# Gates on GpSimd's weight work and slot copies in a fused attention and feed-forward kernel

## The chip, the cores and the metric

The kernel runs on one core of a Trainium2 chip. A core has a matrix engine (TensorE, PE in the profile), a vector engine (VectorE, DVE), a scalar engine (ScalarE, ACT), GpSimd (POOL), and SyncE (SP), which here only issues transfers. Each engine works through its own list of instructions in the order in which the program wrote them, and waits at an instruction until the semaphores it names have come. The metric is the device time of one execution in microseconds; lower is better.

## The reference

The input is 4 sequences of 1024 tokens with 256 features. A block of attention with 16 heads of 16 features and a feed-forward block of three ternary layers follow each other, each between two layer norms and with a residual:

```python
x = L0_attn_x
x = x + _layernorm(_L0_attn_ref(_layernorm(x, axis=-1), L0_attn_Wqkv, L0_attn_Wout), axis=-1)
x = x + _layernorm(_L0_ffn_ref(_layernorm(x, axis=-1), ...), axis=-1)
# attention
scores = jnp.einsum('bhqd,bhkd->bhqk', q, k) * scale
attn = _stable_softmax(scores)          # exp(clip(x - max, -50, 50)) / (sum + 1e-6)
out = jnp.einsum('bhqk,bhkd->bhqd', attn, v)
# feed-forward
h = jax.nn.silu(_tlin(x, w1_w, w1_s)) * _tlin(x, w2_w, w2_s)
h = jax.nn.gelu(_tlin(h, h1_w, h1_s), approximate=False)
h = jax.nn.gelu(_tlin(h, h2_w, h2_s), approximate=False)
return _tlin(h, w3_w, w3_s)
```

## The kernel before

**Two stages.** Attention runs from the start to about 573 us, the feed-forward block from there to the end. The changed lines all act in attention.

**Units and tiles.** Attention is cut into 32 units (b, g, h): sequence b of 4, group g of 4 heads, half h of the queries. In this text unit n is counted from 0, so that n = 8 b + 2 g + h. A unit has 16 score tiles (c, u): 8 key tiles c of 128 tokens, and two pairs of heads u. A score tile is two matmuls (`exponentials`, L554) and one exponential of 128x1024 on ScalarE (L555). The exponentials of a key tile are then weighed with the values in a matmul that accumulates over the 8 key tiles (`weigh`, L562, tile `acc`, one PSUM buffer). At the end of a unit VectorE transposes `acc` to `o` (L824), and the next unit's first `acc` matmul has to wait for that. The exponentials stand in a ring of 8 tiles, and VectorE takes a running maximum over a part of them (`rise`, L574, tile `top`), so that a place in the ring comes free when both have read it.

**Rounds.** The loop at L1464 writes the program round by round: 3 score tiles are made, then the key tiles that are ready are weighed (three halves of a tile, or four where the weighing has fallen behind, and never past a unit's end), then `side.take` at L1501 writes other work. There are 16 rounds in three units. The variable `weighed` tells which score tile is weighed next, and `tiles[weighed][3]` is its c.

**Other work.** `Side` holds chains of `Step`s. A step comes out at the first `take` that is at least `gap` takes after the step before it in its chain, if its `ready()` says yes. Steps that use TensorE come out one at a time, the others freely; within a `take` the chains go in the order in which they were added. So `Side` decides only where in each engine's list an instruction stands. The engine then runs it as soon as its semaphores allow, which can be long before TensorE is at that round.

**What GpSimd does in attention.**

- `round_weights` (6 blocks of w1, w2, w3) and then `round_corners` (16 corners of h1 and h2) form one chain. A corner has three steps: `load` (two transfers into the tile `w`, L309), `plain` (two copies L319 and L320 and a store, L312) and `sums` (four additions or subtractions L327 to L330 and a store). The gaps are 2, 3 and 1. The tile `w` has one buffer, and so has `wr`, which both `plain` and `sums` write: the first addition has to wait until the store of `plain` has landed.
- `slots` copies the values of four heads into `vaug` (L532), two units ahead of their use. `unit_end` writes it, before it adds the chain of `stack`.
- `stack` copies the queries and keys of a group into the tiles `sq` and `sk` that the score matmuls read. These are 32 transfers of 64 KB (L500) in six steps of 6, 6, 6, 6, 6 and 2, one step to a take; every third transfer is issued by GpSimd and the others by SyncE. Of the GpSimd share, the steps have 2, 2, 2, 2, 2 and 1. The last eight transfers, in the last two steps, fill the query stack of u = 1. The first step waits until the queries and keys have been made (`later["qk"]`, `later["qk1"]`), which is late for groups 2.
- The inverse roots of the layer norms (`rstd`, L107) and small squares (`sum`, L432), both behind a VectorE instruction.

The chain of the weights is added before all chains of `stack` but the first, so within one take the weights come first.

Of the kernel before, what the change touches and what calls it, by code (L numbers as in the profile page):

```python
# [73 lines left out]
class Step:  # L74


    def __init__(self, run, gap=0, tensor=True, heavy=False, work=0, split=False):
        self.run, self.gap, self.tensor, self.heavy, self.work, self.split = run, gap, tensor, heavy, work, split
        self.ready = lambda: True


class Norms:
# [61 lines left out]
def tile_fast(ctx: ExitStack, tc: tile.TileContext, x, wqk, wv, wo, w1, w1s, w2, w2s, h1, h1s, h2, h2s, w3, w3s, out, bad):  # L144
# [5 lines left out]
    NT = S // P  # L150
# [62 lines left out]
    with ExitStack() as actx, ExitStack() as rctx:  # L213
# [60 lines left out]
        work = actx.enter_context(tc.tile_pool(name="work", bufs=2, side="right"))  # L274

        def misc(name):
            return ps_misc.tile([P, NQ], F32, tag="misc", name=name)

        def round_weights(n, c):

            st = {}

            def rows(w):
                return w[c * P : (c + rows_at_once[n]) * P, :].rearrange("(i p) d -> p i d", p=P)

            def load():
                st["w"] = work.tile([P, WIDE], F32, tag="w", name="w", bufs=1)
                nc.gpsimd.dma_start(out=st["w"].rearrange("p (i d) -> p i d", i=rows_at_once[n]), in_=rows(weights[n]))

            def cast():  # L290
                st["r"] = work.tile([P, WIDE], F32R, tag="wr", name="wr", bufs=1)
                nc.gpsimd.tensor_copy(st["r"], st["w"])
                nc.gpsimd.dma_start(out=rows(rounded[n]).bitcast(F32), in_=st["r"].bitcast(F32).rearrange("p (i d) -> p i d", i=rows_at_once[n]))

            return [Step(load, 2, False), Step(cast, 4, False)]

        made_factors = [0]

        def round_corners(n, c, x):


            st = {}
            half = NQ // 2

            def load():
                st["w"] = work.tile([P, WIDE], F32, tag="w", name="w", bufs=1)
                rows = weights[n].rearrange("(j c p) (i x n) -> c x p j i n", j=2, p=P, i=2, x=2)[c, x]
                for j in range(2):
                    nc.gpsimd.dma_start(out=st["w"].rearrange("p (j i n) -> p j i n", j=2, i=2)[:, j], in_=rows[:, j])  # L309

            def store(r, k0, k1):
                nc.gpsimd.dma_start(  # L312
                    out=factors[n][k0:k1, :, c, x * half : (x + 1) * half].rearrange("k p n -> p k n").bitcast(F32),
                    in_=r.bitcast(F32).rearrange("p (k n) -> p k n", n=half)[:, : k1 - k0],
                )

            def plain():
                r = work.tile([P, WIDE], F32R, tag="wr", name="wr", bufs=1)
                nc.gpsimd.tensor_copy(r[:, 0:half], st["w"][:, 0:half])  # L319
                nc.gpsimd.tensor_copy(r[:, half : 3 * half], st["w"][:, 2 * half : 4 * half])  # L320
                store(r, 0, 3)

            def sums():
                r = work.tile([P, WIDE], F32R, tag="wr", name="wr", bufs=1)
                s1, s2, s3, s4 = (r[:, k * half : (k + 1) * half] for k in range(4))
                a11, a21, a12, a22 = (st["w"][:, k * half : (k + 1) * half] for k in range(4))
                nc.gpsimd.tensor_tensor(s1, a21, a22, ALU.add)  # L327
                nc.gpsimd.tensor_tensor(s2, s1.bitcast(F32), a11, ALU.subtract)
                nc.gpsimd.tensor_tensor(s3, a11, a21, ALU.subtract)
                nc.gpsimd.tensor_tensor(s4, a12, s2.bitcast(F32), ALU.subtract)  # L330
                store(r, 3, 7)
                made_factors[0] += 1

            return [Step(load, 2, False), Step(plain, 3, False), Step(sums, 1, False)]

        def by_slots(o, w, i, **flags):

# [176 lines left out]
        def stack(b, g):  # L514

            outstanding.append((b, g))

            def done():
                stacked[g % 2] = b, g
                outstanding.remove((b, g))  # L520

            turns = (nc.sync, nc.gpsimd, nc.sync)
            runs = [copy for w in (1, 0) for copy in copies(g, w)]
            steps = few([lambda copy=copy, queue=turns[i % len(turns)]: copy(queue) for i, copy in enumerate(runs)], 2 * len(turns))
            steps[0].ready = lambda: later["qk" if g < GPT else "qk1"] == b
            return steps + [Step(done, 0, False)]

        def slots(b, g, t0=0, t1=NT, engine=nc.gpsimd):


            def run():
                engine.tensor_copy(  # L532
                    vaug[g % 2][:, t0:t1, :, 0:DH], cv[:, t0:t1, HPG * DH * g : HPG * DH * (g + 1)].rearrange("p t (h e) -> p t h e", e=DH)
                )
                slotted[g % 2] = b, g, t1

            return run
# [3 lines left out]
        tiles = [(b, g, h, c, u) for b in range(B) for g in range(NG) for h in range(NH) for c in range(NT) for u in range(2)]  # L541
# [173 lines left out]
        class Side:  # L715


            def __init__(self):
                self.first, self.rest, self.slot = [], [], 0
                self.room, self.open, self.tired = 0.0, None, False  # L720
# [58 lines left out]
        side = Side()  # L779
# [41 lines left out]
        def unit_end(b, g, h):  # L821

            o = both.tile([P, NQ], F32, tag="o", name="o", bufs=2)
            nc.vector.transpose(o, accs[b, g, h])  # L824
            unit = side.add((divide_last if (b, g) == (B - 1, NG - 1) else divide)(g, h, o, tops[b, g, h]), True)
            if b and not g:

                unit[0][-1].ready = lambda: not any(step.tensor for step in ends[b - 1, h][0])
            if g == NG - 1:
                last = ending(b, h, to_scalar if (b, h) == (B - 1, NH - 1) else to_vector)  # L830
                unit[0].extend(last)
                ends[b, h] = unit
            if h < NH - 1:
                return

            n, at = g + 2, b
            if n >= NG:
                n, at = n - NG, b + 1
            if b == B - 1 and g == NG - 2:
                side.add([Step(lambda q=q: load_factor(q), 2 if q else 0, False) for q in range(SLOTS // 2)])  # L840
            if at < B:
                put = Step(slots(at, n), 0, False)
                if at > b:
                    later["chain"][0].append(put)
                else:
                    put.run()
                side.add(stack(at, n))
            if g == NG - 3 and b + 1 < B:
                later["chain"][0].extend(later["rest"])
            elif g == NG - 3:  # L850
                chunks = [(n, [c]) for n in ("w1", "w2") for c in range(DC)]
                loads = [Step(lambda n=n, c=c: load_weights(n, c), 2 if n == "w1" else 1, False) for n, c in chunks]

                loads[0].ready = lambda: not later["flags"][0]
                loads[DC].ready = lambda: not outstanding
                side.add(loads)
                second = prepare(1, to_vector)
                second[-DC].ready = lambda: not outstanding
                side.add([Step(lambda: None, 3, False)] + prepare(0, to_vector) + second)
            if g == NG - 1:  # L860
                begin(b + 1)
# [11 lines left out]
        def load_weights(n, chunks=None):  # L873
            for c in range(len(homes[n])) if chunks is None else chunks:
                nc.sync.dma_start(out=homes[n][c].bitcast(F32), in_=rounded[n][c * P : (c + 1) * P, :].bitcast(F32))

        def load_factor(q):


            if q >= B * 2 * len(order):  # L880
                return
            n, k = square[q // len(order) % 2], order[q % len(order)]
            for i, t in enumerate(ring_of[q % SLOTS]):
                nc.sync.dma_start(out=t.bitcast(F32), in_=factors[n][k, :, 2 * i : 2 * i + 2, :].bitcast(F32))
# [567 lines left out]
        begin(0)  # L1452
        side.add(stack(0, 1) + few(load_rest(), 1))
        side.add([s for k in blocks for s in round_weights(*k)] + [s for k in corners for s in round_corners(*k)])
        made = seen = weighed = half = 0

# [7 lines left out]
        while weighed < len(tiles):  # L1464
            n = end = made
# [3 lines left out]
            if made == len(tiles):  # L1469
                n = made  # L1470
# [274 lines left out]
```

## Time and profile before

| | us |
|---|---|
| median of 3 runs | 1183.34 (1180.86 to 1184.16) |
| profiled execution, device time | 1187.39 |
| profiled execution, span from first to last instruction | 1185.6 |
| attention, first unit's end to last unit's end | 49.7 to 573.5 |
| busy in 45 to 573: PE, ACT, DVE, POOL | 509.1, 485.6, 396.3, 255.1 |
| last store of a corner of the weights begins | 455.67 |

The profiled execution took 1187.39 us, 4.05 us above the median of the runs. "Busy" is the time in which an engine had an instruction under way; for POOL it includes the issuing of its transfers. A wait line reads "engine, tile, line <- what was waited for: us in total, times, longest". A timeline row reads "start in us from the first instruction, us, engine, line, operation, tiles written <- read, shape, count", with the idle time before it in brackets, and what ended it.

### The profile page before, as it was taken

Reading aid. Unit: us, or ns where it says so; the run is one execution under the profiler, and the core shown is the slowest. Engines: PE = TensorE matmul, PEld = TensorE weight load, DVE = VectorE, ACT = ScalarE, POOL = GpSimd, SP = SyncE. Lnnn points to the kernel's source line nnn. Section 1 sums busy time; section 2 is a strip of 40 time slices with the busy share of each in tenths; the row PEclk is TensorE's granted clock in tenths of the full one; section 3 lists DMA queues with packets and bytes.
Section 4 is the critical chain, followed back from the end, with each engine's and each line's share of the span. In section 5 each row is a group of like instructions: output and inputs, shape, how many; then the busy total and the mean of one; then the engine's idle time right before and its main releaser. Section 6 shows DMA issues by size and latency. Waiting matters only on the chain.

```text
span 1185.6 us, 21591 instructions
## 1 busy us (share of the span) xinstructions
PE 1150.1 (97%) x8122; PEld 715.4 (60%) x8122; DVE 847.0 (71%) x1503; ACT 892.9 (75%) x1061; POOL 301.0 (25%) x458
## 2 busy tenths in 40 slices
PE   8999999999999999999999999999999999999996
PEld 3333333334333343333578889888898888988886
DVE  3576578986877876787785756868668686685856
ACT  3899899988998889999467565676756767566664
POOL 6364265674765563220000000000000000000000
PEclk9999999999999999999999999999999999999999
DMA  5865565666646565463304342254622545225421
GB/s 144 221 176 156 142 187 138 185 182 168 164 140 174 153 171 145 100 158 117 108 26 141 119 161 70 91 183 134 196 71 92 176 141 194 73 91 180 138 72 39
DMA packets 78737, 163.68 MB, mean 138 GB/s; under 512 B 14752, under 2 KB 40992, under 8 KB 78624
## 3 DMA queue, kind: packets, MB, share of 16 engines
q1 hardware_dynamic: 62752, 120.05, 34.6%
q0 software_dynamic: 15200, 41.50, 11.8%
q8 instruction: 66, 1.08, 0.4%
q10 hardware_dynamic: 672, 0.66, 0.2%
q14 instruction: 47, 0.39, 0.1%
HBM read 98.71 MB, written 29.88 MB: 108 GB/s over the span
## 4 chain that ended last, share of the span: by engine, by line
PE 77%; ACT 8%; DVE 7%; issue 3%; DMA 2%; SPq 1%; POOL 1%; ACTq 0%; POOLq 0%; DVEq 0%
PE ph L1072 34%; PE acc L562 13%; PE pg L993 9%; PE s L554 8%; ACT e L555 7%; PE pz L1172 5%; PE p L339 3%; PE py L339 2%; PE pv L339 2%; DVE top L574 1%; DVE st L97 1%; SPq L500 1%; PE fpt L936 1%; DMA w<-in_w_dram 1%; DVE xn L140 0%
## 5 line engine op out<-in xcount | busy, mean ns | idle before, releaser
L555 ACT ACTIVATE e<-s 128x1024 f32<-128x1024 f32 x512 | 484.3, 1041 | 44.0 <-PE s L554 36.8
L562 PE MATMUL acc<-e,vaug 128*32 128x512 f32 (+1 forms) x2552 | 255.6, 515 | 1.9 <-DVE o L824 1.8
L107 POOL TENSOR_TENSOR rstd<-ve,minus_half 128x4 f32<-128x4 f32 (+1 forms) x33 | 38.4, 1163 | 679.6 <-DVE ve L105 679.6
L554 PE MATMUL s<-sq,sk 64*128 64x512 f32 x1024 | 187.1, 443 | 18.2 <-ACT e L555 14.6
L554 PEld LDWEIGHTS s<-sq,sk 64*128 64x128 f32 x1024 | 88.1, 185 | 152.6 <-ACT e L555 112.6
L1072 PE MATMUL ph<-hi,sq 128*128 128x512 f32 x448 | 175.7, 392 | 0.0
L1072 PE MATMUL ph<-lo,sq 128*128 128x512 f32 x448 | 174.7, 390 | 0.0
L1072 PE MATMUL ph<-lo,sk 128*128 128x512 f32 x448 | 174.5, 390 | 0.0
L1072 PE MATMUL ph<-hi,sk 128*128 128x512 f32 x448 | 174.4, 389 | 0.0
L574 DVE TENSOR_TENSOR top<-top,e 128x512 f32<-128x512 f32 x192 | 138.8, 723 | 14.2 <-ACT e L555 8.1
L562 PEld LDWEIGHTS acc<-e,vaug 128*32 128x32 f32 x2552 | 66.0, 109 | 122.0 <-issue 107.2
L967 DVE TENSOR_TENSOR lo<-g,hi 128x1024 fp32r<-128x1024 f32 x48 | 58.8, 1224 | 52.4 <-ACT hi L963 52.4
L1072 PEld LDWEIGHTS ph<-lo,sk 128*128 128x128 f32 x448 | 84.2, 188 | 17.5
L1072 PEld LDWEIGHTS ph<-hi,sk 128*128 128x128 f32 x448 | 84.1, 188 | 17.5
L1072 PEld LDWEIGHTS ph<-lo,sq 128*128 128x128 f32 x448 | 84.2, 188 | 17.1
L1072 PEld LDWEIGHTS ph<-hi,sq 128*128 128x128 f32 x448 | 84.1, 188 | 17.1
L1060 ACT ACTIVATE c<-ph,h_scale 128x512 f32<-128x512 f32 x64 | 40.5, 685 | 52.0 <-PE ph L1072 52.0
L995 ACT ACTIVATE sg<-pg,w_scale 128x512 f32<-128x512 f32 x64 | 44.0, 688 | 44.4 <-PE pg L993 38.0
L967 DVE TENSOR_TENSOR lo<-c,hi 128x1024 fp32r<-128x1024 f32 x48 | 58.2, 1220 | 24.2 <-ACT hi L963 24.2
L339 PE MATMUL p<-xT,wqk_sb 128*32 128x512 f32 x512 | 65.7, 593 | 0.5 <-ACT xT L342 0.5
L996 DVE SCALAR_TENSOR_TENSOR g<-pg,w_scale,sg 128x512 f32<-128x512 f32 x64 | 47.8, 748 | 19.9 <-ACT sg L995 19.9
L1172 PE MATMUL pz<-w_sb,lo 128*128 128x256 f32 x256 | 61.6, 283 | 0.0
(199 smaller groups left out, 1848.2 us busy)
## 6 DMA issues: line engine op xcount, KB each, us to landing
sq<-h_f SPq DMA_DIRECT2D x56, 512.0 KB, 4.0
sk<-h_f SPq DMA_DIRECT2D x56, 512.0 KB, 4.7
w<-in_h_dram POOLq DMA_DIRECT2D x32, 256.0 KB, 5.2
h_f<-wr POOLq DMA_DIRECT2D x16, 512.0 KB, 4.0
x<-in_h_dram SPq DMA_DIRECT2D x16, 512.0 KB, 3.5
top_d<-top SPq DMA_DIRECT2D x30, 256.0 KB, 2.6
folded<-top_d SPq DMA_DIRECT2D x30, 256.0 KB, 3.2
h_f<-wr POOLq DMA_DIRECT2D x16, 384.0 KB, 3.6
```

The source lines that it names most:

```text
L339: nc.tensor.matmul(o[j : j + SLOT, :], w[:, j : j + SLOT], i, **flags)
L554: nc.tensor.matmul(s[:, a, :], stacks[1, g % 2, u][r, c * P : (c + 1) * P], stacks[0, g % 2, u][r, h * NQ : (h + 1) * NQ], start=True, sto ...
L555: nc.scalar.activation(pair(k)[:, u], s, AF.Exp)
L562: nc.tensor.matmul(acc[SLOT * i : SLOT * (i + 1), q0:q1], vaug[g % 2][:, c, i, :], pair(k)[:, i // 2, i % 2, q0:q1], start=c == 0 and q0 = ...
L574: nc.vector.tensor_max(top, top if c > 1 else pair(k - 2)[:, :, :, 0:P], pair(k)[:, :, :, 0:P])
L967: nc.vector.tensor_sub(self.lo[i].t, self.raw[i].t, self.hi[i].t.bitcast(F32))
L993: nc.tensor.matmul(p[:, k, :], homes[n][d][:, m * P : (m + 1) * P], half[:, d, :], start=d == j == 0, stop=d == DC - 1 and j == 1)
L995: nc.scalar.activation(sg, p[:, 0, :], AF.Silu, scale=scales["w1"][:, m : m + 1])
L996: nc.vector.scalar_tensor_tensor(x[i, h][c // 2].t[:, c % 2, :], p[:, 1, :], scales["w2"][:, m : m + 1], sg, ALU.mult, ALU.mult)
L1060: nc.scalar.activation(o.t[:, j, :], (o.t if src is None else src)[:, j, :], AF.Gelu, scale=scale[:, m : m + 1])
L1072: nc.tensor.matmul(p[:, j, :], w, half, start=start and c == n == 0, stop=c == HC // 2 - 1 and n == 1, skip_group_check=True,)
L1172: yield c, lambda half=half, c=c, n=n: nc.tensor.matmul(p[:, j, :D], half[:, t * P : (t + 1) * P], homes["w3"][c], start=c == order[0] and ...
```

## The change

A step can be given a `ready` when it is made. The new helper `inside(lead, rest)` says yes while the tile weighed next has a c from `lead` to 8 - `rest`, and always once all tiles are weighed. The casts of blocks, `plain` and the slot copies may come out at c from 0 to 5, `sums` at c from 1 to 4. The slot copy that `unit_end` used to write at once becomes a chain of its own ahead of the chain of `stack`; its gap is now 1 in place of 0, also where it stands at the end of the prologue's chain.

```diff
-    def __init__(self, run, gap=0, tensor=True, heavy=False, work=0, split=False):
+    def __init__(self, run, gap=0, tensor=True, heavy=False, work=0, split=False, ready=lambda: True):
         self.run, self.gap, self.tensor, self.heavy, self.work, self.split = run, gap, tensor, heavy, work, split
-        self.ready = lambda: True
+        self.ready = ready
...
+        def inside(lead, rest):
+            return lambda: weighed == len(tiles) or lead <= tiles[weighed][3] <= NT - rest
+
         def round_weights(n, c):
...
-            return [Step(load, 2, False), Step(cast, 4, False)]
+            return [Step(load, 2, False), Step(cast, 4, False, ready=inside(0, 3))]
...
-            return [Step(load, 2, False), Step(plain, 3, False), Step(sums, 1, False)]
+            return [Step(load, 2, False), Step(plain, 3, False, ready=inside(0, 3)), Step(sums, 1, False, ready=inside(1, 4))]
...
             if at < B:
-                put = Step(slots(at, n), 0, False)
+                put = Step(slots(at, n), 1, False, ready=inside(0, 3))
                 if at > b:
                     later["chain"][0].append(put)
                 else:
-                    put.run()
+                    side.add([put])
                 side.add(stack(at, n))
```

## The prediction

> **What bounds the kernel now.** I read the page first, then the busy time by stage, the waits between 45 and 573 us, and the timelines of the places that these name.
>
> ```profile
> PE 1150.1 (97%) x8122; PEld 715.4 (60%) x8122; DVE 847.0 (71%) x1503; ACT 892.9 (75%) x1061; POOL 301.0 (25%) x458
> ...
> POOL 6364265674765563220000000000000000000000
> ...
> PE 77%; ACT 8%; DVE 7%; issue 3%; DMA 2%; SPq 1%; POOL 1%; ACTq 0%; POOLq 0%; DVEq 0%
> ```
>
> TensorE is busy for 97% and carries 77% of the chain that ended last; GpSimd carries 1%. Its row is filled up to slice 19 only, so the change can act in attention alone. There (45 to 573 us, 528 us) PE is busy for 102.53 + 146.39 + 144.51 + 115.71 = 509.1 us, and ACT for 485.6: PE has about 19 us of idle time, and that is the most that any reordering could win. The waits say who owns it (engine, what for, total us, times, longest):
>
> ```profile
> PE s L554 <- ACT e L555: 13.2, 37, 1.2
> PE s L554 <- DMA sq<-cq1lo: 2.3, 2, 1.8
> PE acc L562 <- DVE o L824: 1.8, 4, 1.0
> ...
> ACT e L555 <- DVE top L574: 5.2, 4, 1.9
> ```
>
> No line has POOL as the one waited for. GpSimd reaches PE in two ways only. First through VectorE, when both want the same operands' port: VectorE is late, then ScalarE, then PE. Second through the transfers that GpSimd issues: the wait for `sq` is one for a stack copy. Both have an instance in the timelines. The first, at the start of units 12 and 21 (ACT):
>
> ```profile
> 240.81 3.77 ACT L555 ACTIVATE e<-s 128x1024 f32<-128x1024 f32 x4 [1.69 <-DVE top L574]
> ...
> 397.93 3.77 ACT L555 ACTIVATE e<-s 128x1024 f32<-128x1024 f32 x4 [1.87 <-DVE top L574]
> ```
>
> At both, GpSimd was at the four operations of `sums` (236.67 to 240.1, 395.01 to 398.4). PE's own idle rows there, found in its list of gaps, are 1.00 us at 241.89 and 1.21 at 399.00, its two longest behind ACT. The second, at the end of unit 19 (PE), and the same place one sequence later, near the end of unit 27 (POOL, SP, PE):
>
> ```profile
> 372.29 1.24 PE L554 MATMUL s<-sq,sk 64*128 64x512 f32 x6 [1.83 <-DMA sq<-cq1lo]
> ```
>
> ```profile
> 495.05 0.57 POOL L432 TENSOR_TENSOR sum<-sum 128x1 bf16<-128x1 f32 x1 [8.70 <-DVE sum L431]
> 495.56 0.53 POOL L500 DMA_DIRECT2D sk<-ck1hi  x1
> 496.08 0.96 POOL L500 DMA_DIRECT2D sq<-cq1hi  x2
> 497.04 0.48 POOL L500 DMA_DIRECT2D sq<-cq1lo  x1
> 497.51 0.48 POOL L500 DMA_DIRECT2D sq<-cq1hi  x1
> 497.99 0.96 POOL L500 DMA_DIRECT2D sq<-cq1lo  x2
> ```
>
> ```profile
> 503.39 2.42 SPq L500 DMA_DIRECT2D sq<-cq1lo  x2
> ```
>
> ```profile
> 507.24 1.81 PE L554 MATMUL s<-sq,sk 64*128 64x512 f32 x6
> ```
>
> Here the stack of (b 3, g 2) is copied. SyncE issues the last two transfers at 503.4 and 504.0, they land in 3.5 us, and the matmuls of the first u = 1 tile start at 508.4. GpSimd's share was issued by 499. So the deadline is met by SyncE with nothing to spare, and GpSimd has some 9 us left.
>
> **What the Trainium skill says.** "SBUF — State Buffer", Who interferes with whom: a VectorE instruction with two SBUF inputs contends with a GpSimd instruction that reads SBUF, and the second to start is held until the first ends. The trace agrees: a `top` takes 649 ns at least and up to 1229, and the operations of L328 to L330 take 730 ns undisturbed and 1180 beside a `top`. "Trainium Kernel Development and Optimization", Key Constraints: transfers of all issuing engines run on the same 16 DMA engines, and issuing from several only saves issue time. In the trace a stack copy costs GpSimd 0.49 us to issue.
>
> **The change part by part.** No instruction is added or removed, and weights and slots have `work` 0 and no TensorE, so the lists of PE, ACT, DVE and SP stay as they are. Only POOL's list is reordered.
>
> *Where the steps go.* By the loop's rule of three or four halves, takes come at c = 0, 2, 4, 5, 7 in units with n divisible by 3, at 0, 2, 3, 5, 6 in the next and at 0, 1, 3, 4, 6, 7 in the one after. The chain of weights starts at the first take. Counting gaps gives for the kernel before one corner in 6 takes, the first `sums` at unit 7, c 5 and the last at unit 24, c 4; the trace has the first at 160.65 (unit 7 runs from 150.7 to 166.4) and the last at 452.44 (unit 24 from 445.5 to 462.2), so the count holds. With the gates I get the `sums` at (unit, c) = (8,1) (9,2) (10,3) (11,4) (13,2) (14,3) (15,4) (17,1) (18,2) (19,3) (20,4) (22,2) (23,3) (24,4) (26,1) (27,2). Five corners are held by 3 takes: the last store moves by 15 takes, 15 x 3.1 us (528 us over 171 takes) = 46 us, from 455.7 to about 502 to 506. The first h factor is asked for at unit 29's end, 545 us, so the weights themselves are not late.
>
> *Slot copies.* In the middle of a sequence they go from the unit's end to the take just behind it (c 0 is allowed): some 0.6 us of work moved by nothing that counts, as `vaug` is used 16 us later. Those for the next sequence move by one take (3.1 us); the tightest was done at 297.85 and needed at 306. Cost 0.
>
> *Gain at the two VectorE stalls.* `sums` at (12,0) and (21,0) go. Worth the PE gaps, 1.00 + 1.21 = 2.2 us (up to ACT's 3.6). But `sums` at (18,2) and (8,1) now stand behind a slot copy that waits for the unit's end, so they run in its first 4 us. At unit 18 the first two `top`s and the product `on` have two SBUF inputs; two collisions at 0.4 to 0.5 us (1.18 - 0.69) make 0.8 us, at unit 8 half as much: +1.3. `sums` at (26,1) delays a `rstd` by some 1.7 us; behind it VectorE has idle gaps of 0.93 and 2.96 us that take it up. Together -0.9 (bounds -4 and +1).
>
> *Stack of (3,2), end of unit 27.* `plain` now comes out at (27,0) and `sums` at (27,2), in front of stack steps 4 and 5 (counted from 0; SyncE's order around the write and read of `top_d` puts these at (27,2) and (27,4)). POOL's list: the `sum` waits for VectorE until 495.05, as before, and stack step 2 is issued by 496.6. `plain`: 1.5 us to its store at 498.1 (1.2 to 2.3 in most corners). Store 0.8 and stack step 3 1.0: to 499.9. `sums` must wait for that store to land: from a store's issue to the first addition, the corners that wait show 2.93 to 4.74, mean 3.6: 501.7. Four operations, with the wait before the store, 4.0 (3.5 to 4.6): 505.7. Store 0.8: 506.5. Step 4 is issued from 506.5 to 507.5, step 5 until 508.0. A stack copy issued right behind such a store landed in 3.0 to 6.3, mostly 4.2: 507.5 + 4.2 = 511.7, where 508.4 was the start: PE is held for 3.3 to 3.5 us (0.6 with every short end, 7.9 with every long one). PE is in order, ACT has no scores left, so the time is lost whole. What is late next: all of unit 28 on, equally.
>
> *Stack of (2,2), end of unit 19.* The same with `plain` (19,2) and `sums` (19,3) in front of steps 4 and 5. The stack step before is issued by 357.8, `plain`'s store at 359.5, `sums` from 363.2 to 367.1, its store to 367.9, step 4 to 368.9, step 5 to 369.4; with 4.2 to 5 us it lands at 373.1 to 373.9, after the 372.29 at which PE went on: +1.2 (0 to 2.5).
>
> *Stack of (1,2).* It has `sums` (10,3) in front, but POOL is ahead there: the last copy is issued at about 220 in place of 227.4, needed at 230.9. Cost 0. The other stacks have 10 us or more between GpSimd's last issue and their use.
>
> Sum: -0.9 + 3.5 + 1.2 = +3.8 us. The profiled execution would go from 1187.39 to 1191.2 (span 1189.4), and the median of the runs from 1183.34 to 1187.1.
>
> **The rivals.** *Nothing that can be told apart (33%):* durations nearer the short ends at the two stacks, and the full gain at the two VectorE stalls: +1.7 + 0.5 - 2.2 = 0, 1183.3. A measurement can't tell this kernel from an unchanged one within 0.3%, 3.5 us. For it: PE's own idle in attention is only 19 us, and much in it is untouched. *Faster (17%):* VectorE is the mechanism, and contention counts for more than the PE gaps show: 3.6 us of ACT at units 12 and 21 and the 1.8 us of PE behind `o`, -5.4, 1178. It decides if the last stack copy's issue begins by about 504.2, since then it lands by 508.4. For that `sums` would have to start 5.8 us earlier (4.0 + 0.8 + 1.0), at 498.4, right behind the store of `plain` at 498.1; no corner that waits for it shows less than 2.9. Against it also stands that only about half of the waits for `o` have GpSimd beside them. *Much slower (5%):* `sums` at its longest in both stacks and a late `rstd` that blocks VectorE at a unit's end: 7.9 + 2.5 - 0.9 = +9.5, and up to 1 for the `rstd`: 1192.8 to 1193.8.
>
> **How the numbers follow.** Forecast (slower, some +2 to +7) 45%, with the much slower case 50% for slower by over 0.3%; 33% within; 17% faster. I take the likeliest case, 1187.1; its own range is 1185 to 1190. For 8 in 10 I leave out a tenth at each end: down into the faster case, 1179.5, and up between the forecast's end and the much slower case, 1191.5.
>
> **What would show it.** Right: SP, PE, DVE and ACT have the same instruction counts; the last corner's store on POOL begins near 502 to 506; PE's wait for DMA on `sq` grows from 2.3 us to 6 or 7, with one of 3 us or more near 508 to 512 and one of about 3 near 373; the ACT waits of 1.69 and 1.87 behind `top` are gone. Wrong: no wait for `sq` in unit 27, for instance because POOL reaches `plain` (27,0) before its `sum`, or because the steps of the stack stand in front of `sums`; then the sign turns. New long waits of VectorE for `rstd` would show a cost that I set at nothing.

## The result, and the profile after

The changed kernel takes 1189.62 us (median of 7 runs, 1187.81 to 1190.31). The kernel before, run beside it, takes 1184.88 (7 runs, 1180.86 to 1187.13; the 1183.34 of the first table was the median of three of these). The ratio is 1.0044 with an interval of 1.0030 to 1.0057: the change makes the kernel slower, by 3.6 to 6.8 us (4.7 between the two medians, 5.2 by the ratio). The forecast was +3.8.

The two profiled executions differ by less, 1189.08 against 1187.39, because the one of before lies 2.5 us above its median and the one of after 0.5 below. From the end of the first unit to the end of the last, attention grows from 523.79 to 526.60 us; the part behind it stays (from there to the end of the span 612.08 before, 611.94 after), and the part ahead of it is 1.0 us shorter in the execution of after. Line numbers of the unit code are 5 higher than before (L554 is now L559).

The page of after, first its busy times, GpSimd's row of slices and the chain:

```profile
PE 1149.0 (97%) x8122; PEld 714.7 (60%) x8122; DVE 845.2 (71%) x1503; ACT 893.2 (75%) x1061; POOL 298.5 (25%) x458
...
POOL 7364346665556464530000000000000000000000
...
PE 73%; DVE 8%; ACT 6%; issue 4%; DMA 4%; POOL 3%; SPq 0%; ACTq 0%; DVEq 0%; POOLq 0%
```

The instruction counts are those of before, so no work was added; the chain has twice as much DMA (2% to 4%) and three times as much GpSimd (1% to 3%). Some of the waits of after between 45 and 575 us (engine, what for, total us, times, longest; `sq<-cq1lo` is a copy of queries into their stack):

```profile
PE s L559 <- ACT e L560: 11.2, 34, 1.1
...
PE s L559 <- DMA sq<-cq1lo: 4.7, 2, 2.8
...
ACT e L560 <- DVE top L579: 2.6, 4, 1.2
PE pt L386 <- DVE bounds L475: 2.5, 2, 1.4
...
PE acc L567 <- DVE o L829: 2.1, 5, 1.0
```

ScalarE's wait for `top` halved (5.2 to 2.6), as meant. TensorE's wait for the stack copies doubled (2.3 to 4.7), and a wait for `bounds` that was not there before costs it 2.5. Units are numbered n = 8b + 2g + h as they are worked on, and (n, c) is a place in a unit, as in the prediction; the stack of (2,2) is that of sequence 2 and group 2. The first of the two waits for `sq`, at the stack of (2,2), in TensorE's timeline of after:

```profile
370.60 1.16 PE L559 MATMUL s<-sq,sk 64*128 64x512 f32 x6 [2.84 <-DMA sq<-cq1lo]
```

The second is at the stack of (3,2), near the end of unit 27. GpSimd's timeline of after shows what made it late:

```profile
495.72 0.81 POOL L317 DMA_DIRECT2D h_f<-wr  x1 [0.30 <-POOL wr L325]
496.53 0.52 POOL L505 DMA_DIRECT2D sq<-cq1hi  x1
497.04 0.50 POOL L505 DMA_DIRECT2D sq<-cq1lo  x1
500.31 0.82 POOL L332 TENSOR_TENSOR wr<-w 128x256 fp32r<-128x256 f32 x1 [2.78 <-DMA h_f<-wr]
...
504.42 0.82 POOL L317 DMA_DIRECT2D h_f<-wr  x1 [0.30 <-POOL wr L335]
505.24 0.51 POOL L505 DMA_DIRECT2D sq<-cq1hi  x1
505.74 0.96 POOL L505 DMA_DIRECT2D sq<-cq1lo  x2
```

Before, all six copies into the query stack were out by 499. Now GpSimd's filler, the work that nobody waits for here, stands inside the stack: the store of `plain` and the four operations of `sums` with their wait of 2.78 us. The last two copies are issued at 505.7 and 506.2. TensorE comes for them at 506.7 and goes on at 508.59 (TensorE's timeline of after):

```profile
508.59 0.87 PE L559 MATMUL s<-sq,sk 64*128 64x512 f32 x2 [1.86 <-DMA sq<-cq1lo]
509.39 2.64 PE L567 MATMUL acc<-e,vaug 128*32 128x256 f32 x16
```

In the kernel before the same 16 matmuls of `acc` took 1.50 us:

```profile
508.98 1.50 PE L562 MATMUL acc<-e,vaug 128*32 128x256 f32 x16
```

The table of stretches says why they take 2.64 here (stretch, its length, busy us and count of PE, PEld, DVE, ACT and POOL; then TensorE's granted clock as a share of its full speed, the DMA share and GB/s):

```profile
506.00:508.00 2.00, 0.73 (x4) 0.31 (x2) 1.61 (x5) 2.00 (x3) 1.75 (x3) 1.00 0.92 313
508.00:510.00 2.00, 1.41 (x10) 0.74 (x14) 1.90 (x8) 1.09 (x2) 0.00 (x0) 0.90 0.04 8
510.00:512.00 2.00, 2.00 (x14) 0.26 (x6) 0.96 (x2) 0.58 (x1) 0.00 (x0) 0.50 0.03 9
512.00:514.00 2.00, 2.00 (x17) 0.94 (x14) 0.00 (x0) 1.20 (x2) 0.00 (x0) 0.75 0.89 204
```

After the wait TensorE runs at half its clock from 509.6 to 513.0. The profile of before has the full clock in all of attention. So the stall costs more than its own 1.86 us: the 3.4 us at half clock are up to 1.7 us more.

A smaller part comes a little earlier and through VectorE. `plain`'s two copies run from 494.46 to 495.43, and VectorE's `den` beside them takes 0.97 us, where it took 0.17 before (VectorE's timeline of after):

```profile
494.48 0.97 DVE L586 SCALAR_TENSOR_TENSOR den<-em,o 128x4 f32<-128x4 f32 x1
```

Behind it ScalarE idles for 0.77 us at 499.85, and TensorE waits 1.15 us for ScalarE at 500.93, where it waited 0.65 before. This is some 0.5 us ahead of the wait for `sq`. The other kernels below that have `plain` at (27,0) show the same rows (`den` 0.96 to 0.97, TensorE's wait 1.14 to 1.15), and the three profiles in which it is held until the stack of (3,2) is out do not (0.17, and 0.64 to 0.65). That `den` is what makes ScalarE late is read from the order of the rows.

The wait for `bounds` comes from the other end of the mechanism, VectorE beside GpSimd. The `sums` that stood at unit 12's start (236.67) stand at (13,2) in the changed list, but GpSimd has nothing to wait for there and reaches them some 10 us ahead of that place, in the second half of unit 12. From 246.56 to 249.68 they run beside VectorE's `folded` and `xn` (VectorE's timeline of after):

```profile
246.62 1.72 DVE L609 TENSOR_TENSOR folded<-folded 128x256 f32<-128x256 f32 x2
...
248.61 1.22 DVE L140 TENSOR_SCALAR xn<-x,mv,rstd 128x256 f32<-128x256 f32 x2
```

Before, the same two rows took 0.81 and 0.69 us:

```profile
249.35 0.81 DVE L604 TENSOR_TENSOR folded<-folded 128x256 f32<-128x256 f32 x2
...
250.44 0.69 DVE L140 TENSOR_SCALAR xn<-x,mv,rstd 128x256 f32<-128x256 f32 x2
```

`bounds`, a small piece of VectorE's work, is behind them, and TensorE waits for it (TensorE's timeline of after):

```profile
251.50 0.63 PE L386 MATMUL pt<-ident,xn 128*128 128x128 f32 x4 [1.40 <-DVE bounds L475]
```

### The profile page after: what moved, and what is told of

The parts are those of the page before. It is cut to its first block, busy times and chain, and to the rows that moved or that the text cites. A ratio compares the mean times of both kernels' runs of the same rounds, so it can differ in the third digit from the quotient of the medians.

```text
span 1187.3 us, 21595 instructions
## 1 busy us (share of the span) xinstructions
PE 1149.0 (97%) x8122; PEld 714.7 (60%) x8122; DVE 845.2 (71%) x1503; ACT 893.2 (75%) x1061; POOL 298.5 (25%) x458
## 4 chain that ended last, share of the span: by engine, by line
PE 73%; DVE 8%; ACT 6%; issue 4%; DMA 4%; POOL 3%; SPq 0%; ACTq 0%; DVEq 0%; POOLq 0%
PE ph L1077 33%; PE acc L567 11%; PE pg L998 9%; PE s L559 7%; ACT e L560 5%; PE pz L1177 5%; PE p L344 3%; PE py L344 2%; DVE top L579 2%; PE pv L344 2%; DMA h_f<-wr 1%; DMA w<-in_h_dram 1%; DVE st L97 1%; DVE lo L972 1%; PE fpt L941 1%
## 5 line engine op out<-in xcount | busy, mean ns | idle before, releaser
L559 PE MATMUL s<-sq,sk 64*128 64x512 f32 x1024 | 185.8, 442 | 18.0 <-ACT e L560 12.5
L559 PEld LDWEIGHTS s<-sq,sk 64*128 64x128 f32 x1024 | 87.9, 185 | 151.0 <-ACT e L560 108.6
```

The source lines that it names most:

```text
L559: nc.tensor.matmul(s[:, a, :], stacks[1, g % 2, u][r, c * P : (c + 1) * P], stacks[0, g % 2, u][r, h * NQ : (h + 1) * NQ], start=True, sto ...
```

## The experiments

Every kernel here computes everything that the kernel before computes; only the order of GpSimd's list, or of the queues, differs. Times are medians with the ratio to the kernel before on the same chip (its medians there 1184.72, 1184.72 and 1184.33) and the ratio's 95% interval. A loss or gain given in us is the ratio times the kernel before; it need not be the difference of the two medians.

**The two halves of the change, each alone.** First the slots' gates without those of the weights:

```diff
-                put = Step(slots(at, n), 0, False)
+                put = Step(slots(at, n), 1, False, ready=inside(0, 3))
...
-                    put.run()
+                    side.add([put])
```

> The slot copies alone are put behind the gate; the weights stay as before. Theory (GpSimd's stack copies wait behind plain and sums at the ends of units 19 and 27): within 1.5 us of the kernel before, PE's wait for sq stays at about 2.3 us. Rival (the slot copies cost the time, by a late vaug or by what they push on GpSimd): slower by 3 to 5 us.

Measured: 1184.94, ratio 1.0005 (0.9995 to 1.0015). Then the weights' gates without the slots':

```diff
-            return [Step(load, 2, False), Step(cast, 4, False)]
+            return [Step(load, 2, False), Step(cast, 4, False, ready=inside(0, 3))]
...
-            return [Step(load, 2, False), Step(plain, 3, False), Step(sums, 1, False)]
+            return [Step(load, 2, False), Step(plain, 3, False, ready=inside(0, 3)), Step(sums, 1, False, ready=inside(1, 4))]
```

> The gates stand on the casts, plain and sums alone; the slot copies stay as before. Theory: as the changed kernel, slower than before by 3.5 to 5.5 us, unit 27 some 3 us longer than before. Rival (slot copies): within 1.5 us of before.

Measured: 1190.66, ratio 1.0063 (1.0044 to 1.0081), with waits for `sq` of 4.6 us. The slot copies alone cost nothing, and the weights alone make the whole loss. Their trace has one wait more (VectorE's timeline of the weights alone):

```profile
349.48 0.77 DVE L140 TENSOR_SCALAR y<-y,mv,rstd 128x256 f32<-128x256 f32 x2 [5.53 <-POOL rstd L107]
```

Here the slot copy of unit 18 stands in front of `plain`, so `sums` and the `rstd` behind it come late, and unit 18 takes 19.43 us against 17.71 in the changed kernel, where the slots' gate puts `plain` first and the longest wait for `rstd` is 0.94. Whether this is why the ratio is higher here (1.0063 against 1.0044 and, below, 1.0034) stays open; the intervals overlap.

**The last corner.** One kernel is the changed one with only the last corner's `plain` (and so its `sums`) held until unit 28, behind the stack of (3,2):

```diff
-Step(plain, 3, False, ready=inside(0, 3))
+Step(plain, 3, False, ready=inside(0, 3) if (n, c, x) != corners[-1] else lambda: weighed >= 28 * 2 * NT and inside(0, 3)())
```

> The changed kernel, but the last corner's plain and sums come out from unit 28 on, so that nothing stands in front of the last two steps of the stack of (3,2). Theory: no wait for sq near 508 us, unit 27 back at 15.2 us from 18.25, so 3 us faster than the changed kernel, still slower than before by 1 to 2.5 us. Rival (the time went to many small delays on VectorE, units 8 to 26): within 1 us of the changed kernel, since unit 27 would then find another wait.

Measured: 1188.67, ratio 1.0038 (1.0023 to 1.0053), +4.5 us, where +1 to +2.5 was expected: a miss. The wait near 508 is gone and unit 27 is back at 15.17 us (before 15.19, after 18.25), but the wait at (2,2) is there with 2.89 us, and in the profiled execution two stretches of half clock follow it, 373.5 to 380.3; a third is at 237. This execution, with 1192.01, is the slowest of the seven runs. Nearly the same order, measured again further down as "(2,2) left", lost 2.9 us. The converse is the kernel before with the last corner alone moved into the stack of (3,2):

```diff
-Step(plain, 3, False), Step(sums, 1, False)
+Step(plain, 3, False, ready=lambda: (n, c, x) != corners[-1] or weighed >= 27 * 2 * NT), Step(sums, 1, False, ready=lambda: (n, c, x) != corners[-1] or tiles[weighed][3] >= 2)
```

> The kernel before, in which the last corner's plain and sums alone are moved to units 27, c 0 and c 2; nothing else moves. Theory: PE waits for sq near 508 us for about 2 us, unit 27 is 3 us longer, slower than before by 2.5 to 3.5 us. Rival: within 1 us of before.

Measured: 1188.47, ratio 1.0036 (1.0025 to 1.0047), +4.3 us. TensorE's timeline of this kernel:

```profile
509.15 0.82 PE L554 MATMUL s<-sq,sk 64*128 64x512 f32 x2 [2.11 <-DMA sq<-cq1lo]
```

One corner's filler, placed in front of three copies, makes a loss about as large as the whole change's.

**The stacks first.** This is the changed kernel with one more condition: `plain` and `sums` also wait while a stack of the two late groups is outstanding.

```diff
+            def late():
+                return any(at > 1 and at < B and g == GPT and later["qk1"] == at for at, g in outstanding)
...
-Step(plain, 3, False, ready=inside(0, 3)), Step(sums, 1, False, ready=inside(1, 4))
+Step(plain, 3, False, ready=lambda: inside(0, 3)() and not late()), Step(sums, 1, False, ready=lambda: inside(1, 4)() and not late())
```

> The changed kernel, but plain and sums are also held while the stack of (2,2) or of (3,2) is being copied; every other gate stays. Theory (the loss is the stack copies behind sums): faster than the changed kernel by 4 to 5.5 us, so within 1.5 us of before, or up to 2 us faster for the two waits of ScalarE at units 12 and 21 that the gates remove; no wait for sq near 508, the one near 372 at most as before. Rival (the loss is contention on VectorE at the new places, with PE's new waits for bounds at 251 and 390 us as its sign): within 1.5 us of the changed kernel.

It ran beside the unaltered changed kernel once more:

> The changed kernel once more, on the chip of the next three, so that they can be set beside it: slower than before by 4 to 6 us.

Measured: stacks first 1185.07, ratio 0.9999 (0.9986 to 1.0012); the changed kernel 1189.35, ratio 1.0034 (1.0021 to 1.0047). The whole loss is recovered. GpSimd's timeline with the stacks first:

```profile
492.00 0.57 POOL L441 TENSOR_TENSOR sum<-sum 128x1 bf16<-128x1 f32 x1 [1.21 <-DVE sum L440]
492.51 0.53 POOL L509 DMA_DIRECT2D sk<-ck1hi  x1
...
494.94 0.96 POOL L509 DMA_DIRECT2D sq<-cq1lo  x2
...
504.36 0.51 POOL L324 CAST wr<-w 128x256 fp32r<-128x256 f32 x1
```

and its waits:

```profile
PE s L563 <- DMA sq<-cq1lo: 1.0, 1, 1.0
...
PE pt L390 <- DVE bounds L479: 1.4, 1, 1.4
```

The six copies are out in one piece and the filler follows 8.5 us later. The wait for `bounds` at unit 12 is still there while the time is back, so this collision on VectorE is not the loss. The other wait for `bounds`, 1.11 us at 389.59 in the changed kernel, is gone: the hold at (2,2) also moves the `sums` that stood beside it, from (20,4) to (21,2). What is ascribed to the stack of (2,2) below contains this wait.

**One stack at a time.** The same condition for the stack of (2,2) alone (`at == 2`), and for (3,2) alone (`at == 3`). The second leaves (2,2) as in the changed kernel. The first leaves filler in the stack of (3,2), but not at the same place: the hold delays the chain, so that the last `plain` stands at (27,2) and the last `sums` at (27,4), in front of three copies and of one.

> The changed kernel, with plain and sums held during the stack of (2,2) alone; the last corner still stands in front of the stack of (3,2). Theory, from the unit lengths of the profiles: 1 to 2.5 us faster than the changed kernel (unit 19 and the wait for bounds in unit 20), unit 27 as in the changed kernel; so 2 to 3.5 us slower than before. Rival, after the held last corner gave so little: the stack of (2,2) carries nearly all, and this is within 1 us of before.

> The changed kernel, with plain and sums held during the stack of (3,2) alone. Theory: 2.5 to 4 us faster than the changed kernel (units 26 and 27), so 1 to 2.5 us slower than before. Rival: as with the held last corner, less than 1 us faster than the changed kernel.

Measured: with (3,2) left 1188.38, ratio 1.0029 (1.0017 to 1.0041), +3.4 us; with (2,2) left 1187.95, ratio 1.0025 (1.0013 to 1.0036), +2.9 us. TensorE's timelines, of the one that leaves (3,2):

```profile
507.25 0.65 PE L563 MATMUL s<-sq,sk 64*128 64x512 f32 x1 [1.76 <-DMA sq<-cq1lo]
```

and of the one that leaves (2,2):

```profile
371.98 1.24 PE L563 MATMUL s<-sq,sk 64*128 64x512 f32 x6 [2.64 <-DMA sq<-cq1lo]
```

Each stack costs by itself. Their sum, 6.3 us, is above the 4.0 and 5.2 of the changed kernel's two sets of runs; the intervals allow equality, and whether the two costs add is not settled.

**The gain by itself.** The kernel before, with the four `sums` that began at a unit's start moved one take on (and the next load brought one take nearer):

```diff
-            return [Step(load, 2, False), Step(plain, 3, False), Step(sums, 1, False)]
+            k = corners.index((n, c, x))
+            off = (3, 4, 11, 12)
+            return [Step(load, 1 if k - 1 in off else 2, False), Step(plain, 3, False), Step(sums, 2 if k in off else 1, False)]
```

> The kernel before, in which the four sums that stood at c 0 (units 11, 12, 20, 21) come out one take later and the next load takes one take less, so that all the other steps stay where they were. The gain that I booked for the gates, alone: ScalarE's waits of 1.69 and 1.87 us behind top at the starts of units 12 and 21 go, 1.5 to 2.5 us faster. If VectorE's lateness there is taken up elsewhere: within 1 us of before.

Measured: 1183.94, ratio 0.9993 (0.9986 to 1.0000): 0.8 us faster, with an interval from 1.7 to nothing, where 1.5 to 2.5 was expected. The two places are the right ones: in the profiles unit 12 goes from 17.72 to 16.70 us and unit 21 from 19.28 to 18.23, together 2.1 us. Why the runs show less than that is open.

**An even split of the copies.** In the kernel before SyncE was the late one at (3,2) (its last copy landed at 507.53, GpSimd's at 502.82), so the stacks of the late groups were divided evenly between SyncE and GpSimd:

```diff
-            turns = (nc.sync, nc.gpsimd, nc.sync)
+            turns = (nc.sync, nc.gpsimd, nc.sync) if g != GPT else (nc.sync, nc.gpsimd)
```

> The kernel before, in which the stacks of the groups 2 are issued half by GpSimd and half by SyncE, in place of one third and two thirds; nothing else changes. If the stacks' last copies are what PE waits for at the end of unit 19, that wait goes: faster by 1 to 2.5 us, with fewer runs at the slow end. If that wait is an accident of the profiled execution: no change.

Measured: 1187.47, ratio 1.0010 (0.9996 to 1.0023): a miss, no gain. The waits at (2,2) fall from 0.44 and 1.83 to 0.71 and 0.23 us, but waits of 0.83 at 129.35 and 0.76 at 234.06 appear at the earlier stacks. In the other profiles in which no weight work was moved into this stack, the waits at (2,2) are 0.54 to 1.25 in all. So a good part of the 2.27 belonged to that one profiled execution, which is the second of the outcomes named above.

**Both lessons together.** The kernel before, with `plain` and `sums` held while a late stack is outstanding, and `sums` never at a unit's start; no other gate:

```diff
-Step(plain, 3, False), Step(sums, 1, False)
+Step(plain, 3, False, ready=lambda: not late()), Step(sums, 1, False, ready=lambda: not late() and tiles[weighed][3] > 0)
```

> Not a test but a version made of what the runs showed: the kernel before, in which plain and sums are held during the stacks of (2,2) and (3,2), and sums does not come out at c 0; no other gate, slot copies as before. If the gains add up (0.8 us for sums away from c 0, and up to 2 us at the stack of (2,2)): 1 to 2.5 us faster than before. If the stack of (2,2) waits for SyncE alone: 0.5 to 1 us faster.

Measured: 1182.07 (1179.65 to 1183.34), ratio 0.9974 (0.9962 to 0.9985), 2.3 us of 1184.33 less than before: the fastest of all kernels here. Its wait for stack copies is as long as that of the moved `sums` alone (0.96 us), so it isn't shown that the hold at the stacks is what gains:

```profile
PE s L558 <- DMA sq<-cq1lo: 1.0, 1, 1.0
```

**The books.** Unit lengths, from the end of one unit to the end of the next in each profiled execution, put the waits and the clock side by side. The waits are those in the units named. "Half clock" says how often the profile has TensorE at half clock in these units for some 3.4 us.

| kernel | unit 27 | wait for `sq` there | half clock | units 19+20 | wait for `sq` there | half clock |
|---|---|---|---|---|---|---|
| before | 15.19 | 0 | no | 35.76 | 2.27 | no |
| slots alone | 15.18 | 0 | no | 33.71 | 0.54 | no |
| `sums` moved alone | 15.15 | 0 | no | 34.76 | 0.96 | no |
| stacks first | 15.16 | 0 | no | 35.29 | 1.0 | no |
| last corner alone | 16.83 | 2.11 | no | 35.99 | 1.1 | once |
| last corner held | 15.17 | 0 | no | 39.50 | 2.89 | twice |
| weights alone | 16.83 | 2.04 | no | 37.98 | 2.60 | once |
| after | 18.25 | 1.86 | once | 37.18 | 2.84 | no |
| after, again | 18.45 | 2.04 | once | 37.66 | 3.29 | no |
| (3,2) left | 18.35 | 1.76 | once | 35.32 | 1.25 | no |
| (2,2) left | 15.15 | 0 | no | 38.20 | 2.64 | once |

In unit 27 a wait of about 2 us alone makes 1.7 us, and the same wait with a stretch of half clock 3.1 to 3.3. Over units 26 to 28, which take in the delay behind `den` too, it is 2.0 and 2.5 us without the half clock and 3.4 to 4.0 with it, against the 50.02 us with the stacks first. (The kernel that leaves (3,2) has 53.38 there: 3.4 us more, which is its whole loss in the runs.) Against the kernel with the stacks first, the changed kernel's second profile has 5.9 us more of attention (527.25 and 521.37). Waits for `sq` are 4.3 of it (5.3 less 1.0), the half clock 1.7, waits for `bounds` 1.1 (2.5 less 1.4), and unit 5, whose length changes from execution to execution, gives 1.25 back: 5.85. For the kernel that leaves (3,2) the same sum is 2.0 + 1.7 - 1.26 = 2.4, measured 2.5; for the one that leaves (2,2) it is 1.6 + 1.7 + 1.1 - 1.2 = 3.2, measured 2.2, a microsecond off.

The runs without a full profile bear it out through their mean granted clock: 0.9962 before, and 0.9939 and 0.9948 in the two sets of the changed kernel. Of a span of 1187 us these differences are 2.7 and 1.7 us. For the kernels that leave (3,2) and (2,2) they are 2.8 and 1.2 us, for the last corner alone 0.9, and with the stacks first 0.2. Read so, the half clock is a fifth of the loss with the last corner alone and most of it where (3,2) is left. This is bookkeeping over runs that were made for something else; no kernel here switched the half clock on or off by itself, so that it is part of the loss is read from traces, not shown by an edit.

## Why the prediction was right, and where it was not

**The sign, the place and nearly the size were right.** +3.8 was forecast, +4.7 measured between the medians (3.6 to 6.8). Two terms of the sum were too low, by 0.9 and 1.7 us (below), and the two stacks measured alone add up to more than the whole change, so that the total came this close is in part luck. Of the 2.5 us between 1187.1 and 1189.62, 1.5 are that the kernel before itself reads 1184.88 over seven runs and not 1183.34.

**Where the steps go: right.** All 16 `sums` stand in GpSimd's list at the (unit, c) that the count of takes gave, and the last store was issued at 504.42, where 502 to 506 was forecast.

**Slot copies at 0: right**, by the slots alone (1.0005).

**`rstd` at 0: right for this order.** VectorE's longest wait for it is 0.94 us, as it was before. The step "No line has POOL as the one waited for" had passed over VectorE's three waits for `rstd`, 2.2 us in the same list, and in the weights alone one of them grew to 5.53 us.

**Stack of (3,2), +3.5: right in the sum, wrong in two of its terms.** Held alone it is worth 3.4 (the one that leaves it) or 4.3 us (the last corner alone). But the landing was taken as 4.2 us behind a large store and was 2.7 to 3.0 for the last three copies, so TensorE stood for 1.8 to 2.1 us and not 3.3 to 3.5. What filled the gap was not in the sum at all: the step "PE is in order, ACT has no scores left, so the time is lost whole" ended the loss where TensorE went on, and TensorE went on at half clock, up to 1.7 us; some 0.5 came through VectorE's `den`. For the same reason the forecast wait for `sq`, 6 to 7 us, was too large (4.7 measured), while the time was right. That the errors of this term are of nearly the same size and cancel is luck.

**Stack of (2,2), +1.2: wrong in size; 2.9 measured.** The step compared the new landing with "the 372.29 at which PE went on" in the profile of before. That execution already held a wait of 1.83 us there and lay 2.5 us above its median. In the profiles of the slots alone and of the moved `sums`, which issue this stack as before, units 19 and 20 take 33.71 and 34.76 in place of 35.76. The wait was thus charged only for its growth over an unusually bad case. The half clock was missing here too, and so was the wait of 1.11 us for `bounds` in unit 20.

**VectorE, -0.9 net: the size fell, not the mechanism.** The two waits behind `top` did go (1.69 gone, 1.87 down to 0.56 at 395.99), and units 12 and 21 together fell from 37.00 to 35.84. The 2.2 us were too much: the starts of these units alone are worth 0.8 in the runs (nothing to 1.7). The losses were sought at units 8 and 18. Unit 18 showed a new wait of 0.65 behind `top`; the larger ones came where the working had not looked, `folded` and `xn` beside the `sums` of (13,2) and (20,4), and TensorE's 1.40 and 1.11 us for `bounds`. With the stacks held, all that is left of the gates is worth 0.9999 (0.9986 to 1.0012). So the term was about zero, apart from the wait of 1.11 us that went with the hold.

**Contention and the clock.** The Trainium skill's "SBUF — State Buffer", Who interferes with whom, carried the VectorE terms, and the new places agree: `folded`, which has two SBUF inputs, goes from 0.81 to 1.72 us a pair beside `sums`. `xn`, which has one large input and is not the case that the prediction drew on, goes from 0.69 to 1.22. What I had not used is the skill's "TensorE: Matmul & The Clock Gate", Part 1: TensorE's clock is halved after an idle window of about 3.4 us, and these windows run freely, whatever the kernel does. The traces agree on the half (0.50) and on the length (3.4 us), and the grid stands elsewhere in each execution (first stretch at 24.9 us in one, at 27.0 in another). They do not agree that the window must be idle; the last section has the numbers.

**The rivals.** "Nothing" needed short ends at the stacks and the full gain of 2.2 us; each stack alone costs 2.9 us or more and the gain is 0.8, so it fell. "Faster" needed the last copy's issue to begin by 504.2, and it began at 506.2, although this execution was 1.6 us ahead of the profile of before at this place. "Much slower" needed the longest `sums` in both stacks, and they took 3.8 us from 500.31 to 504.12.

## What to carry to other kernels

An engine that nobody waits for can still hold deadlines, because the transfers that it issues stand in one list with its filler work: before filler is moved, find the last issue of each transfer that has a deadline, and hold the filler by the outstanding transfers rather than by the phase of a loop. Price a stall of TensorE by what follows it as well as by its length (here up to 1.7 us behind a wait of 1.86), and look at its granted clock in the stretch behind. Where one profiled execution lies above its median, ask which waits are its own before a change is priced against them.

## What the runs showed of the hardware

**Half clock after partly idle windows.** Within one execution, the stretches of half clock begin a whole number of 3.413 us apart: in the changed kernel at 24.9 and 509.6 (142.0 of them), with the last corner held at 25.4, 237.0 and 373.5 (62.0 and 102.0). I laid this grid over ten profiled executions that have such a stretch at their start to place it, and summed TensorE's busy time in each window of attention. Nine windows had 1.66 us or less of 3.41; after seven of them the next window ran at half clock. One of the seven, with the slots alone at 130.8, had no matmul at all; the other six had 1.26 to 1.66 us. In these executions no window with 1.84 to 2.32 us busy was followed by one, and only two above that were (2.33, and 2.68 in a window that already ran at half clock). So the price of a wait of 2 us seems to depend on where it falls on this grid, which no run here moved on purpose. The kernel before had 1.83 us of waiting at 370.5 to 372.3, divided over two windows with 2.23 and 2.77 busy, and kept its clock; the changed kernel's 1.86 us at 506.7 lay inside one, with 1.55 busy, and lost it. The two low windows without a loss (1.53 and 1.65, both in the changed kernel at (2,2)) and the one at 2.33 stay unexplained, and so does a stretch at 368.4 in the last corner alone, behind 1.1 us of waiting and a window with 2.29 busy. Busy time in one window is thus not the whole rule.

**The clock goes with much of the spread from run to run.** In three sets of 41, 42 and 36 runs of the kernel before, the time falls by 1.1, 0.9 and 1.4 us for each 0.001 of mean granted clock (correlations -0.79, -0.63 and -0.84); 0.001 of the span is 1.2 us. A correlation doesn't say which of the two is the cause.

**Lengths repeat closely.** Most units agree to 0.1 us between executions of kernels that don't differ there. Unit 5, which waits for the transfer of `folded`, takes 18.25 to 23.93 us, in kernels that all order it alike or nearly so. (The 23.93 is the execution of the slots alone, in which VectorE waited 8.08 us for that transfer.)
